# Moving three kinds of stores from SyncE's queue to ScalarE's in a graph network kernel

## The chip, the cores and the metric

The kernel runs on one core of a Trainium2 chip. The metric is the device time of one execution in microseconds (us); the time given for the kernel is the median of several executions, and one further execution was recorded by the hardware profiler. Engines are named as the profile names them: PE (TensorE; PEld is its weight load), DVE (VectorE), ACT (ScalarE), POOL (GpSimd) and SP (SyncE). Each has its own queue of instructions and works through it in order. A DMA is started by an instruction in the queue of SP, ACT or POOL; "SPq" and "ACTq" mark such rows in a timeline.

## The reference, cut to what matters

Four graph layers work on 6250 nodes with 256 features each and 106250 edges sorted by destination. Each adds its result to its input and normalizes the rows.

```python
edge_index = jnp.stack([src, dst])
x = _layernorm(x + _L0_gnn_ref(x, edge_index, L0_gnn_weight, L0_gnn_attn_l, L0_gnn_attn_r), axis=-1)
x = _layernorm(x + _L1_gnn_ref(x, L1_gnn_W, edge_index), axis=-1)
x = _layernorm(x + _L2_gnn_ref(x, edge_index, edge_weight, L2_gnn_W1, L2_gnn_b1, L2_gnn_W2, L2_gnn_b2), axis=-1)
x = _layernorm(x + _L3_gnn_ref(x, L3_gnn_W, edge_index), axis=-1)
```

The first is an attention over single edges. The other three are of the form "multiply the node features by a matrix, scale, gather the row of each edge's source, add it up at the destination, scale". The third does this twice. So there are four aggregations; the last one aggregates at the source and is taken as a dense product with the adjacency matrix of the graph.

## The kernel before, in words

Nodes are cut into 49 blocks of 128, edges into 831 tiles of 128. The function `sorted_edges` holds everything that follows; its order is written out by hand (`tc.manual_schedule()`), so each engine runs its instructions in the order in which the Python code emits them. Generators are used to interleave parts: each `yield` marks a place at which another part may put in its instructions.

**The front** (to 266 us) loads, counts degrees, and computes the attention in seven groups of seven blocks. For each group, `end` (L844 on) scales seven blocks on ACT into tiles `h0` (L856), of which there are four, and stores each as 128 rows of the first table in HBM, `tables[0]` (L857); then ACT writes the normalized blocks in place (L860), and one store of the whole group follows (L862). ACT also takes the square root of each group (L310) and the exponential (L825), whose function tables are loaded in between.

**Aggregation** (`aggregate`) is called for three layers, here called layers 0, 1 and 2. It runs over steps of four edge tiles: 155 steps in layer 0, 208 in each of the others. In a step POOL starts four gathers (L953), each bringing 128 rows of a table into one of 16 tiles `g`. PE multiplies each with a one-hot tile into `agg` (L960). ACT copies that to `part` (L963). In the next step, PE multiplies `part` with a second one-hot tile (L924), and DVE adds the result into a ring of accumulators (L929). When a block of nodes is complete, a `finish` generator runs on it: matrix product (L305), scaling, normalization on DVE with a square root on ACT (L310). In layer 0, `rest1` ends with a store of the normalized block (L1078, on SP), a scaling on ACT into `row` (L1081) and the store of `row` into the second table, `tables[1]` (L1082).

**Beside layers 0 and 1** runs `build`, which makes the dense adjacency matrix block by block. Per step of the aggregation it is advanced 2.75 times (layer 0) or 2.95 times (layer 1). It has two kinds of pieces. `count` makes one-hot tiles on DVE (L503, L506), multiplies them on PE into PSUM tiles `pa` (L527), which ACT casts into one of two tiles, `AT` and `big` (L531), while DVE adds up a count from the same PSUM tile (L533). `use` takes the finished block: for the last 13 blocks of nodes it first multiplies it with the table in dense form (L547, 147 matmuls in seven pieces), then it turns the block in ten pieces of up to five 128x128 tiles: PE transposes into a PSUM tile `tp` (L559), ACT copies it to one of three tiles `ac` (L563), and a DMA stores 160 KB into `adj` in HBM (L564). The tiles `pa`, `tp` and one more kind share three PSUM buffers; the function `behind` puts off the emptying of each until the next piece has been emitted, so ACT empties one while PE fills the next. The blocks that need the dense product come first in `order`, so all of them fall into layer 0.

Loads of the kernel's own rows (`fetch`, L991), of edges for `build` (L434) and all stores but POOL's are in SP's queue, in the order of emission. All DMAs of SP and ACT take turns on eight semaphores, and each waits until the one before it on its semaphore has landed.

**Layer 2** has the dense product with `adj` beside it (L1195, loads L1165) and a tail of dense products alone. The layers are tied together by their tables: the first gather of a layer waits until all stores of its table have landed.

Of the kernel before, what the change touches and what calls it, by code (L numbers as in the profile page):

```python
# [23 lines left out]
P = 128  # L24
# [219 lines left out]
def sorted_edges(ctx, gr, x, src, dst, edge_weight, w0, attn_l, attn_r, w1, w2a, b2a, w2b, b2b, w3,  # L244
# [8 lines left out]
    V, S, G, T, SY = nc.vector, nc.scalar, nc.gpsimd, nc.tensor, nc.sync  # L253
# [28 lines left out]
    tables = [dram.tile([NP, D], F32, name=f"h{i}") for i in range(3)]  # L282
# [3 lines left out]
    adj = dram.tile([NB, P, NP], BF, name="adj")  # L286
# [26 lines left out]
    def rsqrt_end(y, d, s):  # L313

        V.reciprocal(y, s)
        V.tensor_mul(s, y, y)
        V.tensor_mul(s, s, d)
        V.tensor_scalar(s, s, -0.5, 1.5, op0=OP.mult, op1=OP.add)
        V.tensor_mul(y, y, s)
# [92 lines left out]
    def build(bg, ps, more, finish_dense):  # L412
# [70 lines left out]
        def behind(empty=None):  # L483
            while pending:
                pending.pop(0)()
            if empty:
                pending.append(empty)
# [50 lines left out]
        def use(b, AT):  # L538

            behind()  # L540
            if b >= NS1:
                while not parted:
                    yield
                acc = ps.tile([P, D], F32, name="da", bufs=1)
                for k in range(NB):
                    for j in range(3):
                        T.matmul(acc, AT[:, k, :], HP[:, k, j, :], start=k == 0 and j == 0,  # L547
                                 stop=k == NB - 1 and j == 2)
                    if k % SB == SB - 1:
                        yield  # L550
                more.append(finish_dense(b, acc))

            V.tensor_add(AT[:, b, :], AT[:, b, :], ident_b)

            for k0 in sorted(range(0, NB, KC), key=lambda k: k <= b < k + KC):
                n = min(KC, NB - k0)
                tp = ps.tile([P, KC, P], BF, name="tp", tag="w", bufs=3)
                for k in range(n):
                    T.transpose(tp[:, k, :], AT[:, k0 + k, :], ident_b)  # L559

                def empty(tp=tp, k0=k0, n=n):
                    ac = bg.tile([P, KC, P], BF, name="ac", bufs=3)
                    S.copy(ac[:, :n, :], tp[:, :n, :])  # L563
                    SY.dma_start(adj[b, :, k0 * P:(k0 + n) * P], ac[:, :n, :].rearrange("p k q -> p (k q)"))  # L564

                behind(empty)
                yield
# [36 lines left out]
    with one_order:  # L604

        with tc.tile_pool(name="first", bufs=1) as ft, \
# [186 lines left out]
            row = ft.tile([1, P], F32, name="row")  # L793
# [50 lines left out]
            def end(i, mv, va, s):  # L844

                rs = wk.tile([P, GB, 2], F32, name="rstd")
                sh = wk.tile([P, GB, 2], F32, name="sh")
                rsqrt_end(rs[:, :, 0], va, s)
                V.scalar_tensor_tensor(sh[:, :, 0], mv[:, :, 0], -1.0, rs[:, :, 0], op0=OP.mult, op1=OP.mult)
                d = dis1[:, i * GB:(i + 1) * GB]  # L850
                V.tensor_mul(rs[:, :, 1], rs[:, :, 0], d)
                V.tensor_mul(sh[:, :, 1], sh[:, :, 0], d)
                for j in range(GB):
                    b = i * GB + j
                    h = wk.tile([P, D], F32, name="h0", bufs=4)
                    S.activation(h, X[:, b, :], AF.Identity, bias=sh[:, j, 1:2], scale=rs[:, j, 1:2])  # L856
                    SY.dma_start(tables[0][b * P:(b + 1) * P, :], h)  # L857
                for j in range(GB):
                    b = i * GB + j
                    S.activation(X[:, b, :], X[:, b, :], AF.Identity, bias=sh[:, j, 0:1],  # L860
                                 scale=rs[:, j, 0:1])
                SY.dma_start(xs[0][i * GB * P:(i + 1) * GB * P, :].rearrange("(b p) d -> p b d", p=P),  # L862
                             X[:, i * GB:(i + 1) * GB, :])
# [6 lines left out]
            for i in range(ng):  # L870
                if i + 3 < ng:
                    gather_ext(i + 3)
                if i + 2 < ng:
                    gather_alt(i + 2)
                zm = begin(i)
                if last:
                    end(*last)
                last = i, *middle(i, *zm)
            end(*last)

        with tc.tile_pool(name="acct", bufs=1) as ap, tc.tile_pool(name="gat", bufs=16) as gat, \
# [163 lines left out]
            def normalized(y):  # L1045
                mv, va = norm_begin(y, 1)
                yield
                s = rsqrt_begin(va, [P, 1])
                yield
                norm_end(y, y, 1, mv, va, s)  # L1050
# [22 lines left out]
            def rest1(b, ph, xr):  # L1073
                y = fin.tile([P, 1, D], F32, name="y", bufs=3)
                V.scalar_tensor_tensor(y[:, 0, :], ph, dis1[:, b:b + 1], xr, op0=OP.mult, op1=OP.add)
                taken.pop()
                yield from normalized(y)
                SY.dma_start(xs[1][b * P:(b + 1) * P, :], y[:, 0, :])  # L1078
                yield
                row = fin.tile([P, D], F32, name="row")  # L1080
                S.activation(row, y[:, 0, :], AF.Copy, scale=dis2[:, b:b + 1])  # L1081
                SY.dma_start(tables[1][b * P:(b + 1) * P, :], row)  # L1082

            def finish1(b):
                assert weighed
                xr, o = fetch(xs[0], b, "xr"), own(b)
                yield
                yield from bank()
                ph = sums(b, W1)
                yield  # L1090
                yield from rest1(b, ph, xr)
                yield from follow(b, o)

            def finish_dense(b, acc):
                xr = fetch(xs[0], b, "xr")
                a = fin.tile([P, D], F32, name="h")
                S.copy(a, acc)
                yield
                xT = yield from transposed(a)
                yield from bank()  # L1100
                ph = times(ps, xT, W1, tag="ep")
                yield
                yield from rest1(b, ph, xr)
                joined.append(b)
# [543 lines left out]
```

## Time and profile before

| | us |
|---|---|
| median of 3 runs | 3590.57 |
| the runs | 3584.35 to 3593.58 |
| the profiled execution | 3590.18 |
| its span, first to last instruction | 3588.3 |
| first gather of layer 0 | 266.3 |
| last gather of layer 0, first of layer 1 | 1118.7, 1135.5 |
| last adjacency store | 2168.1 |
| last gather of layer 1 | 2216.0 |
| last gather of layer 2 | 3280.5 |

The page of the profile gives the busy time of each engine, the same in 40 slices of the span, the DMA queues, the chain of work that ended last, and the costliest groups of instructions. A group's line names the line of code, the engine, the operation, what is written from what, the shape and how often; after the first bar stand the busy time and the mean duration of one in ns, after the second the idle time of the engine just before them and what ended it. A line of waits names who waited for whom, then the sum in us, how many times, and the longest. A line of a timeline has its start, its length in us, engine, line and operation, and in brackets the idle time before it and what ended that. DMA-issuing instructions are not counted as busy.

### The profile page before, as it was taken

Reading aid. Unit: us, or ns where it says so; the run is one execution under the profiler, and the core shown is the slowest. Engines: PE = TensorE matmul, PEld = TensorE weight load, DVE = VectorE, ACT = ScalarE, POOL = GpSimd, SP = SyncE. Lnnn points to the kernel's source line nnn. Section 1 sums busy time; section 2 is a strip of 40 time slices with the busy share of each in tenths; the row PEclk is TensorE's granted clock in tenths of the full one; section 3 lists DMA queues with packets and bytes.
Section 4 is the critical chain, followed back from the end, with each engine's and each line's share of the span. In section 5 each row is a group of like instructions: output and inputs, shape, how many; then the busy total and the mean of one; then the engine's idle time right before and its main releaser. Section 6 shows DMA issues by size and latency. Waiting matters only on the chain.

```text
span 3588.3 us, 64967 instructions
## 1 busy us (share of the span) xinstructions
PE 2824.3 (79%) x22576; PEld 1987.6 (55%) x22576; DVE 1965.7 (55%) x6286; ACT 1057.4 (29%) x2424; POOL 2382.0 (66%) x2424
## 2 busy tenths in 40 slices
PE   5607679999997777777777775588898888889998
PEld 4402356666664444444444443366677676667887
DVE  4575876565667767676767662234444334333333
ACT  1261343333335444444444441121111111111000
POOL 3657467777776777777777776777777777774000
PEclk7558789999999989999989995599999999999999
DMA  5244455555555555555555554477777777665554
GB/s 150 64 155 119 133 162 160 159 165 158 171 173 165 166 162 168 164 164 166 166 164 164 164 164 146 118 248 247 246 243 237 239 234 228 214 203 179 174 185 136
DMA packets 390822, 630.21 MB, mean 176 GB/s; under 512 B 67788, under 2 KB 299603, under 8 KB 390453
## 3 DMA queue, kind: packets, MB, share of 16 engines
q0 software_dynamic: 114288, 307.59, 30.5%
q1 hardware_dynamic: 275090, 315.19, 26.7%
q8 instruction: 179, 2.93, 0.3%
q10 hardware_dynamic: 1104, 3.19, 0.2%
q14 instruction: 161, 1.31, 0.1%
HBM read 469.36 MB, written 157.64 MB: 175 GB/s over the span
## 4 chain that ended last, share of the span: by engine, by line
PE 36%; DMA 20%; issue 6%; DVE 3%; POOL 2%; ACT 2%; SPq 1%; DVEq 0%; ACTq 0%; POOLq 0%
DMA g<-h,e_srci 18%; PE acc L1195 18%; PE agg L960 6%; PE pa L527 5%; PE agq L924 2%; POOL g L953 2%; PE mm L305 2%; PE tp L559 1%; ACT ac L563 1%; PE own L1014 1%; DMA adj<-ac 1%; DMA xr<-x 1%; SPq L434 1%; PE da L547 0%; SPq L430 0%
## 5 line engine op out<-in xcount | busy, mean ns | idle before, releaser
L953 POOL DMA_INDIRECT g<-h,e_srci x2282 | 2240.9, 982 | 773.5 <-issue 328.9
L1195 PE MATMUL acc<-XP,ad 128*128 128x256 bf16 x7203 | 849.8, 279 | 6.1 <-DMA ad<-adj 6.1
L1195 PEld LDWEIGHTS <-ad 128*128 128x128 bf16 x7203 | 704.1, 100 | 182.0 <-issue 82.8
L527 PE MATMUL pa<-ok,olb 128*128 128x400 bf16 (+1 forms) x2352 | 574.9, 372 | 144.7 <-ACT ac L563 73.1
L960 PE MATMUL agg<-g,oh 128*32 128x256 f32 x4564 | 402.5, 427 | 316.7 <-DMA g<-h,e_srci 315.8
L963 ACT COPY part<-agg 128x256 f32<-128x256 f32 x571 | 212.3, 372 | 1487.0 <-PE agg L960 1468.3
L929 DVE TENSOR_TENSOR ACCT<-ACCT,agq 128x128 f32 x571 | 163.8, 287 | 882.2 <-PE agq L924 878.3
L527 PEld LDWEIGHTS <-olb 128*128 128x128 bf16 x2352 | 221.1, 103 | 405.8 <-issue 176.3
L506 DVE TENSOR_SCALAR ok<-it,key 128x784 bf16<-128x784 f16 x1176 | 440.7, 432 | 0.0
L924 PEld LDWEIGHTS agq<-oq,part 128*128 128x128 f32 x2284 | 346.0, 206 | 59.3 <-ACT part L963 25.8
L924 PE MATMUL agq<-oq,part 128*128 128x64 f32 x2284 | 352.0, 280 | 14.8 <-ACT part L963 10.4
L563 ACT COPY ac<-tp 128x640 bf16<-128x640 bf16 (+1 forms) x490 | 333.0, 697 | 63.4 <-DMA adj<-ac 49.1
L960 PEld LDWEIGHTS agg<-g,oh 128*32 128x32 f32 x4564 | 93.6, 112 | 385.9 <-DMA g<-h,e_srci 339.3
L533 DVE TENSOR_TENSOR cnt_s<-cnt_s,pa 128x49 f32<-128x49 f32 x392 | 79.4, 203 | 261.7 <-ACT AT L531 147.8
L531 ACT CAST AT<-pa 128x400 bf16<-128x400 f32 (+1 forms) x400 | 192.1, 499 | 92.6 <-PE pa L527 90.9
L503 DVE TENSOR_TENSOR olb<-it,key 128x384 bf16<-128x384 f16 x392 | 216.7, 553 | 4.5 <-issue 4.3
L531 ACT CAST big<-pa 128x400 bf16<-128x400 f32 (+1 forms) x384 | 183.5, 501 | 90.9 <-PE pa L527 89.3
L380 PE MATMUL pc<-oh,sel_f 128*17 128x392 f32 x136 | 48.8, 510 | 120.7 <-DVE oh L374 120.7
L559 PEld LDWEIGHTS <-AT 128*128 128x128 bf16 x1225 | 86.6, 103 | 95.6 <-issue 81.1
L559 PEld LDWEIGHTS <-big 128*128 128x128 bf16 x1176 | 83.4, 104 | 88.4 <-issue 72.0
L559 PE MATMUL tp<-ident_b,AT 128*128 128x128 bf16 x1225 | 113.5, 231 | 23.0 <-ACT ac L563 20.9
L310 ACT ACTIVATE rs<-va 128x1 f32<-128x1 f32 (+2 forms) x118 | 24.8, 210 | 358.5 <-DVE va L332 358.3
(265 smaller groups left out, 2897.9 us busy)
## 6 DMA issues: line engine op xcount, KB each, us to landing
adj<-ac SPq DMA_DIRECT2D x441, 160.0 KB
ad<-adj SPq DMA_DIRECT2D x96, 640.0 KB
g<-h,e_srci POOLq DMA_INDIRECT x2282
l<-pre SPq DMA_DIRECT2D x60, 512.0 KB
pre<-l SPq DMA_DIRECT2D x60, 512.0 KB
own<-h SPq DMA_DIRECT2D x147, 128.0 KB
xr<-x SPq DMA_DIRECT2D x98, 128.0 KB
x<-y SPq DMA_DIRECT2D x98, 128.0 KB
```

The lines of the kernel that those rows point to most:

```text
L503: V.tensor_tensor(t, it[:, None, :n].to_broadcast([P, CAP, n]), key[:, k, :, None].to_broadcast([P, CAP, n]), op=OP.is_equal)
L506: V.tensor_scalar(ok[:, i, :KW], it, key[:, 0, i:i + 1], None, op0=OP.is_equal)
L527: T.matmul(pa[:, :c - c0 * GR], ol[:, j, :], ok[:, j, c0 * GR:c], start=j == 0, stop=j == CAP - 1)
L531: S.copy(AT[:, c0:c1, r * GR:(r + 1) * GR], pa[:, :m].rearrange("p (k g) -> p k g", g=GR))
L559: T.transpose(tp[:, k, :], AT[:, k0 + k, :], ident_b)
L563: S.copy(ac[:, :n, :], tp[:, :n, :])
L924: T.matmul(p2[:, h, :], part[:m, h * P:(h + 1) * P], oq[:m, q % 2, :], start=True, stop=True)
L929: V.tensor_add(ACT_[:, :, ds(c, WQ)], ACT_[:, :, ds(c, WQ)], p2)
L953: G.indirect_dma_start(out=g, out_offset=None, in_=table, in_offset=bass.IndirectOffsetOnAxis(ap=e_srci[:, t:t + 1], axis=0))
L960: T.matmul(p1[j * W:(j + 1) * W, :], hots[q // 2][0][:, q % 2 * Q4 + j, :], gs[j], start=True, stop=True)
L963: S.copy(part[:n * W, :], p1[:n * W, :])
L1195: T.matmul(acc[:, k, :], ad[:, (b - b0) % BC, k * P:(k + 1) * P], HP[:, b, j, :], start=b == b0 and k % 2 == 0 and j == 0, stop=b == b1 - ...
```

## The change

Three store instructions are given to another queue, each to that of the engine whose instruction stands just ahead of it in the code. Data, sizes, buffers and the order of emission stay as they are. On ACT, 588 DMA-issuing instructions are added (490 of L564, 49 of L857, 49 of L1082), and SP's queue has as many fewer. PE, DVE and POOL have the same instructions in the same order.

```diff
                 def empty(tp=tp, k0=k0, n=n):
                     ac = bg.tile([P, KC, P], BF, name="ac", bufs=3)
                     S.copy(ac[:, :n, :], tp[:, :n, :])
-                    SY.dma_start(adj[b, :, k0 * P:(k0 + n) * P], ac[:, :n, :].rearrange("p k q -> p (k q)"))
+                    S.dma_start(adj[b, :, k0 * P:(k0 + n) * P], ac[:, :n, :].rearrange("p k q -> p (k q)"))
...
                     h = wk.tile([P, D], F32, name="h0", bufs=4)
                     S.activation(h, X[:, b, :], AF.Identity, bias=sh[:, j, 1:2], scale=rs[:, j, 1:2])
-                    SY.dma_start(tables[0][b * P:(b + 1) * P, :], h)
+                    S.dma_start(tables[0][b * P:(b + 1) * P, :], h)
...
                 row = fin.tile([P, D], F32, name="row")
                 S.activation(row, y[:, 0, :], AF.Copy, scale=dis2[:, b:b + 1])
-                SY.dma_start(tables[1][b * P:(b + 1) * P, :], row)
+                S.dma_start(tables[1][b * P:(b + 1) * P, :], row)
```

## The prediction

> **What bounds the kernel now.** I read the page's busy times and slices first, then its cost groups, then waits and windows stage by stage, because the average shares mix stages with different limits.
>
> ```profile
> PE 2824.3 (79%) x22576; PEld 1987.6 (55%) x22576; DVE 1965.7 (55%) x6286; ACT 1057.4 (29%) x2424; POOL 2382.0 (66%) x2424
> L953 POOL DMA_INDIRECT g<-h,e_srci x2282 | 2240.9, 982 | 773.5 <-issue 328.9
> L563 ACT COPY ac<-tp 128x640 bf16<-128x640 bf16 (+1 forms) x490 | 333.0, 697 | 63.4 <-DMA adj<-ac 49.1
> ```
>
> POOL's 66% hides a gap of 0.30 us after each gather: 2282 x (0.982 + 0.30) = 2926 us of a 3588 us span. Gathers, four to a step of the aggregation loop, run from 266 us to 3281 us, so this is the pacemaker unless something else holds it. The window table says where that is (columns: PE, PEld, DVE, ACT, POOL busy, granted clock, DMA share, GB/s).
>
> ```profile
> 450.00:1118.00 668.00, 597.35 (x5086) 423.55 (x5086) 422.52 (x1506) 265.73 (x632) 497.80 (x507) 0.97 0.57 166
> 1135.00:2170.00 1035.00, 766.44 (x5791) 450.67 (x5791) 707.72 (x2261) 481.32 (x1034) 792.90 (x794) 0.90 0.56 165
> ```
>
> Layer 0 (first row): 507 gathers x 0.30 + 497.8 = 650 of 668 us; PE is busy for 89%. Layer 1 (second): 794 x 0.30 + 792.9 = 1031 of 1035, so POOL is full, with PE at 74%. Who waits for whom in the two windows, layer 0 in the first fence, layer 1 in the second:
>
> ```profile
> POOL g L953 <- PE agg L960: 33.1, 56, 3.9
> PE tp L559 <- ACT ac L563: 19.9, 13, 3.5
> PE pa L527 <- ACT ac L563: 17.3, 24, 1.9
> ACT ac L563 <- DMA adj<-ac: 15.8, 8, 5.6
> ```
>
> ```profile
> PE agg L960 <- DMA g<-h,e_srci: 168.2, 118, 3.6
> PE pa L527 <- ACT ac L563: 53.7, 99, 1.6
> ```
>
> In layer 0 POOL waits for PE to free a gather buffer (33.1 us, of which 56 x 0.30 is the ordinary gap), and PE never has a gather wait of note: PE's queue, and what PE waits for, sets the pace. In layer 1 PE waits 168 us for gathers. I also compared each step's first gather with the matmul that freed the buffer it takes (16 gathers back): the margin has a median of 2 to 5 us with minima of 0.3 in layer 0, and 12 to 13 us in layer 1. After 2168 us there is no store of the moved kinds; layer 2 and the dense tail have nothing to change.
>
> **The change, part by part.** 490 adjacency stores (L564), 49 rows of the first table (L857) and 49 of the second (L1082) leave SP's queue and enter ScalarE's, each behind the instruction that made its data. No other engine's order changes.
>
> *What SP loses* is worth little. SP issued them in 0.32 us (median) and otherwise waited for ScalarE (788.5 us for `ac`); SP is no bound. What its order did cost is lateness: behind a store of a normalized row (L1078) that waits for VectorE, adjacency stores went out over 1 us late for 31 of 156 copies before 1118 us, and ScalarE then waited for a buffer: the 15.8 us above (49.1 in all, the other 33.3 in layer 1). A store issued right behind its copy lands after 2.6 us (median here, 4.0 at the 95th percentile), and its buffer is wanted three copies later, over 4 us on. I let all 15.8 us go.
>
> *What ScalarE gains.* The timeline of one step with two transposed tiles, layer 0:
>
> ```profile
> 714.11 0.35 ACT L963 COPY part<-agg 128x256 f32<-128x256 f32 x1
> 714.36 1.29 ACT L563 COPY ac<-tp 128x640 bf16<-128x640 bf16 x2
> 715.08 0.91 SPq L564 DMA_DIRECT2D adj<-ac  x2
> 715.11 0.71 PE L527 MATMUL pa<-ok,olb 128*128 128x433 bf16 x3 [1.18 <-ACT ac L563]
> 715.53 0.90 ACT L531 CAST big<-pa 128x400 bf16<-128x400 f32 x2
> 715.70 0.44 PE L559 MATMUL tp<-ident_b,AT 128*128 128x128 bf16 x5
> ```
>
> Two copies of 0.70 us take 1.29 because the second starts 0.59 after the first; the casts follow just as closely. With a store between, the next instruction waits for the copy's end (0.11 lost), 0.026 until the issue (as SP's row shows), 0.34 for the issue (mean of the 490 rows on SP) and about 0.06 to start again (the step from a wait row to its copy at 1086.4 us): **0.54 us per store**. Bounds: the issue alone, 0.32; and 0.8, if it takes on ScalarE twice the 0.36 us of its one comparable store (L754). Two rules of the Trainium skill bear here. "DMA: Bandwidth & Descriptors" (Issuing engines are not separate DMA queues) says that queues of different engines end on the same 16 DMA engines and that spreading them saves only issue time, usually small beside the transfer. By that rule, 0.32 beside 2.6 us, the change is worth about nothing and the time stays 3591; but the rule weighs an issue against its transfer, and here it is weighed against a step in which PE already waits for ScalarE. "Perfetto Trace Analysis" (DMA Instruction — HWDGE) has the semaphore wait of such a DMA in the sequencer, while computing instructions wait in a queue of their own: nothing behind the store is made ready. That speaks for 0.54 against 0.34; with 0.34, layer 0's sum below would be 30 us and not 48.
>
> *Layer 0, on the path.* Of 129 steps in the window (from one step's first L960 matmul to the next), 41 have no `ac` copy and run the dense matmuls L547 (6.23 us each, PE full); 33 have one copy; 55 have two or three (4.34 us for the 49 without dense matmuls). Behind the first store stand the second `ac` copy, two casts and the next `part`. PE's second transposition at 715.70 starts 0.05 after the second copy ends, so it comes 0.54 later: 55 x 0.54 = 30 us. With one copy, the casts and `xT` come later, and only part of that reaches PE (VectorE's count L533 waits for the casts, the own-matmul for `xT`): half, 33 x 0.27 = 9. Of 43 row stores 35 fall into steps with copies, where the row can stand just ahead of `part`: half again, 9. Together 48, against nothing if PE's other waits cover all, and 103 if every one of 144 + 47 stores passes on fully. Less 15.8 for the ended buffer waits, less 3 of margin at the gathers, plus 4 for the 18 stores of 400 to 450 us, where PE is behind too: **+33 us**, from -16 to +91.
>
> *Ahead of layer 0.* The last group of seven rows runs from 257.54 to 261.47 us (3.93), and POOL's first instruction of the layer (265.08) waits for the ScalarE pass behind it. With 0.59 + 0.026 + 0.32 + 0.06 = 1.0 each, seven take 7.0: +3.1, and the buffer waits of 0.36 go inside it. The groups before have the same +3.1, of which idle time at the next square root covers 1.28 and 1.93 us (its waits at 242.85 and 255.85); earlier ones end in a 6.5 us wait for gathers and cost nothing. Two groups carry about 3 to the last: **+6 us**, 0 to 9.
>
> *End of layer 0.* From the last gather (1118.71) to the next layer's first (1135.48) POOL waits for the last row store, issued at 1132.84, right after its row, as it would be from ScalarE. A few adjacency stores in that chain: **+1**.
>
> *Layer 1: nothing.* 329 stores x 0.54 = 178 us at the very most, over 201 steps 0.88 each; PE's wait for gathers is 0.84 per step and 12 us stand in the buffers. Without that cover each 0.1 us per step costs 20 us.
>
> *Waits that the change could add.* Eight DMA semaphores go round all stores and loads of both queues in program order, so a store on ScalarE waits for the landing of the eighth DMA before it, often SP's. In this trace that DMA had landed at least 0.96 us before each of the 526 stores after 450 us (median 6 and more), and 6.7 before the earlier ones, so I take 0. Behind it would be queued everything that feeds PE.
>
> Sum: 6 + 33 + 1 = 40. 3588.3 + 40 = 3628; the profiled execution took 1.9 beyond its span and was 0.4 below the median: **3631 us**.
>
> **Rivals.**
> *Hidden anyway.* PE's waits in layer 0 cover the stores, and POOL's own pitch (650 of 668 us) sets the layer; only the front pays. For: POOL is within 18 us of full. Against: PE's margin is used up at minima of 0.3 us. 3591 + 6 = 3597.
> *The buffer waits were the price.* ScalarE idles 235 us in layer 0 waiting for `agg`, so issues fall into idle time and only the ended 15.8 us count, the front being absorbed too: 3591 - 16 = 3575. It decides when less than about a sixth of the 103 us reaches PE. Against: the copies stand back to back just where PE waits for them.
> *A dearer issue.* At 0.8 us per store and full passing, layer 1's steps need 5.2 - 0.84 + 1.6 x 0.8 = 5.64 us against POOL's 5.19: +90 there, layer 0 half as much again (+55): about 3740. With half passing, layer 1 is still hidden.
> That the stores stay on SP is excluded by the order of instructions: 588 of them stand in ScalarE's queue.
>
> **How the numbers follow.** 0.3% (11 us) is about what a measurement here can tell from no change. Chances: likeliest case 0.65 (its own range 3612 to 3660: 0.34 us per store and less passing, or 70% passing), hidden 0.14, faster 0.10, dearer 0.11. Slower by over 0.3%: 0.65 + 0.11 and a little of the hidden case, 0.78; same 0.12; faster 0.10. The range leaves out the faster case and the upper part of the dearest: 3595 to 3675.
>
> **What would show it.** Right: `pa` and `tp` waits for `ac` in layer 0 well above 37 us; steps with two copies near 4.9 us; the `ac` wait for `adj` near 0; first gather near 272 us, the layer's last near 1157; layer 1's length within 5 us of 1081; POOL waiting longer for `agg`. Wrong: a layer 0 not longer, ScalarE waiting at a store for another DMA, a store issue far from 0.34 us, or layer 1 no longer held by POOL.

## The result, and the profile after

The changed kernel takes 3637.95 us (median of 4 runs, 3627.68 to 3640.35), the kernel before 3591.84 (median of 4) on the same chip. The estimated ratio is 1.0133, 95% interval 1.0111 to 1.0155, or 48 us (40 to 56) more; the two medians lie 46 apart. The prediction was 3631 us.

The page of the changed kernel, the three lines that were shown of before:

```profile
PE 2841.5 (78%) x22576; PEld 1994.1 (55%) x22576; DVE 1965.9 (54%) x6286; ACT 1090.2 (30%) x2424; POOL 2395.4 (66%) x2424
L953 POOL DMA_INDIRECT g<-h,e_srci x2282 | 2255.2, 988 | 806.2 <-issue 325.9
L563 ACT COPY ac<-tp 128x640 bf16<-128x640 bf16 (+1 forms) x490 | 338.1, 690 | 49.6 <-ACT ac L563 22.5
```

POOL's idle time before gathers has gone from 773.5 to 806.2 us. A copy into `ac` costs what it did (690 ns against 697), but no longer waits for its buffer's store: what it waits for most is now the copy ahead of it on its own engine, which is a wait that the kernel before did not have.

The profiled execution took 3640.35 us with a span of 3638.6, 50.3 more than before. By the times of the first and last gathers, the 50.3 are:

| stretch | before | after | difference |
|---|---|---|---|
| to the first gather of layer 0 | 266.3 | 269.4 | +3.1 |
| layer 0, first to last gather | 852.4 | 888.6 | +36.2 |
| gap to layer 1 | 16.8 | 18.3 | +1.5 |
| layer 1 | 1080.6 | 1088.4 | +7.8 |
| gap, layer 2 and tail | 1372.2 | 1373.8 | +1.6 |

Layer 0 and layer 1 in the table of windows (columns as before: PE, PEld, DVE, ACT, POOL busy, granted clock, DMA share, GB/s):

```profile
453.00:1158.00 705.00, 613.98 (x5082) 431.51 (x5081) 421.92 (x1501) 275.23 (x630) 500.49 (x506) 0.94 0.54 156
1176.00:2265.00 1089.00, 794.10 (x5918) 462.78 (x5919) 717.00 (x2289) 501.20 (x1043) 835.63 (x831) 0.89 0.55 162
```

Layer 0 is 37 us longer with the same work in it. PE's idle time there is 705 - 613.98 = 91.0 us, where it was 70.7 (+20.4), and PE's busy time itself has grown by 16.6, with the granted clock at 0.94 instead of 0.97. Layer 1 is 8 us longer, and POOL's busy time has grown by as much (the window of before in the prediction is narrower; over 1135 to 2216 us POOL was busy for 827.7, by a row shown below).

Who waits for whom in layer 0 after the change, 453 to 1158 us, POOL and PE first, ScalarE in the second fence:

```profile
POOL g L953 <- PE agg L960: 70.7, 73, 4.2
...
PE pa L527 <- ACT ac L563: 16.1, 23, 1.7
PE tp L559 <- ACT ac L563: 15.7, 16, 2.4
PE mm L305 <- ACT xT L1040: 11.9, 11, 1.7
PE tp L559 <- DVE cnt_s L533: 9.7, 5, 2.4
PE pa L527 <- DVE cnt_s L533: 8.8, 13, 3.4
...
PE tp L559 <- ACT big L531: 4.7, 11, 0.5
PE own L1014 <- ACT h L1097: 4.4, 6, 1.4
PE tp L559 <- ACT AT L531: 3.8, 10, 0.5
```

```profile
ACT AT L531 <- ACT ac L563: 11.9, 29, 0.7
ACT ac L563 <- ACT ac L563: 9.9, 22, 0.5
```

And before, 450 to 1118 us, the lines of PE that neither the prediction nor this text has shown yet:

```profile
PE pa L527 <- DVE cnt_s L533: 9.8, 12, 3.6
...
PE mm L305 <- ACT xT L1040: 3.9, 9, 0.9
PE tp L559 <- DVE cnt_s L533: 2.6, 2, 2.0
...
PE own L1014 <- ACT h L1097: 1.4, 3, 0.5
```

POOL waits more than twice as long for PE to free a gather buffer (33.1 us before). The waits point to ScalarE: casts and copies now stand still behind the copy ahead of them. But PE's waits for `ac` itself have not grown: 31.8 us against 37.2. The lateness reaches PE by what ScalarE does after the copies: the wait for `xT` has gone from 3.9 to 11.9 us, the two for the count `cnt_s` together from 12.4 to 18.5, that for `h` from 1.4 to 4.4; the waits of `tp` for the casts, 4.7 us for `big` and 3.8 for `AT`, were not among those of before. Together these have grown by about 25 us; less the 5.4 of `ac`, this is about the 20.4 us of new idle time.

In layer 1, 1176 to 2265 us, PE still waits for gathers first (168.2 us before, in the narrower window):

```profile
PE agg L960 <- DMA g<-h,e_srci: 174.6, 113, 4.5
```

Last the timeline of a step with two copies (start, length, engine, line):

```profile
724.04 0.70 ACT L563 COPY ac<-tp 128x640 bf16<-128x640 bf16 x1
724.77 0.33 ACTq L564 DMA_DIRECT2D adj<-ac  x1
...
725.19 0.69 ACT L563 COPY ac<-tp 128x640 bf16<-128x640 bf16 x1 [0.45 <-ACT ac L563]
725.91 0.33 ACTq L564 DMA_DIRECT2D adj<-ac  x1
725.93 0.44 PE L559 MATMUL tp<-ident_b,AT 128*128 128x128 bf16 x5 [0.43 <-ACT ac L563]
```

The copy ends at 724.74, the store goes out at 724.77 and takes 0.33, the next copy starts 1.15 us after the first one did instead of 0.59: 0.56 us per store. This step is no exception: in layer 0 the 38 pairs of copies that follow each other start 1.15 us apart in the median, the 33 pairs of before 0.58. All 588 stores go out 0.03 us after the end of the instruction that made their data, and of 513 stores on ScalarE from 460 to 2200 us not one lies beside a running instruction of ScalarE.

### The profile page after: what moved, and what is told of

The parts are those of the page before. It is cut to its first block, busy times and chain, and to the rows that moved or that the text cites. A ratio compares the mean times of both kernels' runs of the same rounds, so it can differ in the third digit from the quotient of the medians.

```text
span 3638.6 us, 64214 instructions
## 1 busy us (share of the span) xinstructions
PE 2841.5 (78%) x22576; PEld 1994.1 (55%) x22576; DVE 1965.9 (54%) x6286; ACT 1090.2 (30%) x2424; POOL 2395.4 (66%) x2424
## 4 chain that ended last, share of the span: by engine, by line
PE 50%; DMA 20%; DVE 7%; issue 7%; ACT 5%; POOL 2%; ACTq 1%; SPq 0%; DVEq 0%; POOLq 0%
DMA g<-h,e_srci 18%; PE acc L1195 18%; PE agg L960 8%; PE pa L527 8%; PE da L547 6%; PE agq L924 4%; PE mm L305 3%; ACT ac L563 2%; POOL g L953 2%; PE tp L559 2%; PE pc L380 1%; DMA xr<-x 1%; DVE ok L506 1%; PE own L1014 1%; ACT AT L531 1%
## 5 line engine op out<-in xcount | busy, mean ns | idle before, releaser
L953 POOL DMA_INDIRECT g<-h,e_srci x2282 | 2255.2, 988 | 806.2 <-issue 325.9
L1195 PE MATMUL acc<-XP,ad 128*128 128x256 bf16 x7203 | 849.3, 279 | 6.2 <-DMA ad<-adj 6.2
L1195 PEld LDWEIGHTS <-ad 128*128 128x128 bf16 x7203 | 703.6, 100 | 181.0 <-issue 81.3
L527 PE MATMUL pa<-ok,olb 128*128 128x400 bf16 (+1 forms) x2352 | 588.0, 379 | 152.4 <-ACT ac L563 74.2
L960 PE MATMUL agg<-g,oh 128*32 128x256 f32 x4564 | 403.4, 428 | 305.6 <-DMA g<-h,e_srci 304.5
L960 PEld LDWEIGHTS agg<-g,oh 128*32 128x32 f32 x4564 | 93.8, 113 | 374.0 <-DMA g<-h,e_srci 323.0
L531 ACT CAST AT<-pa 128x400 bf16<-128x400 f32 (+1 forms) x400 | 184.7, 488 | 134.4 <-PE pa L527 90.5
```

The costliest lines, as they stand in the source:

```text
L527: T.matmul(pa[:, :c - c0 * GR], ol[:, j, :], ok[:, j, c0 * GR:c], start=j == 0, stop=j == CAP - 1)
L531: S.copy(AT[:, c0:c1, r * GR:(r + 1) * GR], pa[:, :m].rearrange("p (k g) -> p k g", g=GR))
L953: G.indirect_dma_start(out=g, out_offset=None, in_=table, in_offset=bass.IndirectOffsetOnAxis(ap=e_srci[:, t:t + 1], axis=0))
L960: T.matmul(p1[j * W:(j + 1) * W, :], hots[q // 2][0][:, q % 2 * Q4 + j, :], gs[j], start=True, stop=True)
L1195: T.matmul(acc[:, k, :], ad[:, (b - b0) % BC, k * P:(k + 1) * P], HP[:, b, j, :], start=b == b0 and k % 2 == 0 and j == 0, stop=b == b1 - ...
```

## The experiments

Four sets of runs, each on one chip together with the kernel before. On two of the four chips the kernel before took about 4475 us instead of 3590; what is measured there is compared only there. In the tables, layers 0 and 1 are the times from the first to the last gather in the one profiled execution of each kernel.

**One kind of store at a time, on a chip with another pace.** Each of the first three makes one of the three edits of the change: e1_adj that of L564, e2_h0 that of L857, e3_row that of L1082. The fourth moves no store and only takes ScalarE's time.

```diff
# e4_pad
                     S.copy(ac[:, :n, :], tp[:, :n, :])
+                    S.copy(ac[:, :2, :], ac[:, :2, :])
```

> Only the 490 adjacency stores (L564) move to ScalarE; both kinds of table rows stay on SP. Theory 'time on ScalarE' (each store holds ScalarE for about half a us, and in layer 0 PE has to wait for it): of the 36 us that layer 0 grew in the changed kernel, about 28 here, the front 0, so about 3591 + 30 to 38 = 3621 to 3629. Rival 'the rows do it' (row stores stand just ahead of the copy to part, which PE needs next): less than 15 us over the kernel before. Layer 1 is 1081 us from first to last gather if the 8 us that it grew in the changed kernel were chance, 1088 if the adjacency stores on ScalarE's queue made them.

> Only the 49 rows of the first table (L857) move. First gather at 269.4 us instead of 266.3, as in the changed kernel, and nothing behind it: 3591 + 3 = 3594, not to be told from the kernel before. The prediction had 6 us for this part; if the two earlier groups of seven rows had really carried their delay over, the first gather would come at 272.

> Only the 49 rows of the second table (L1082) move. Theory 'time on ScalarE': 34 of them stand in steps with copies, at half a us and half passing on: layer 0 +9, in all 3600. If the copy to part never waits for a row store, or PE has it late anyway: 3591. Rival 'the rows do it': over 3610.

> All stores stay on SP; after each copy into ac ScalarE copies 256 of its columns onto themselves, which holds ScalarE about as long as issuing a store (0.06 to start, some 0.4 us), and the store waits for it. Theory 'time on ScalarE': layer 0 grows by as much as with the adjacency stores moved or more, since the waits for late stores stay: 3591 + 30 to 50. Rival 'the queue' (what costs is ScalarE's own DMA ring, two queues that share the engines or the eight semaphores): within 10 us of the kernel before. Layer 1 stays at 1081 us by the rival reading of its 8 us as an effect of the queue, and by chance too; 1088 if mere time on ScalarE makes them.

Measured against 4473.94 us (4440.82 to 4499.19) of the kernel before on this chip:

| | median, us | ratio (95%) | layer 0, us | layer 1, us |
|---|---|---|---|---|
| e1_adj | 4440.26 | 0.9930 (0.9907 to 0.9953) | 1063.8 | 1368.3 |
| e2_h0 | 4477.74 | 1.0011 (0.9992 to 1.0029) | 1089.7 | 1374.2 |
| e3_row | 4462.47 | 0.9979 (0.9958 to 1.0000) | 1082.6 | 1380.1 |
| e4_pad | 4462.11 | 0.9984 (0.9959 to 1.0009) | 1078.7 | 1384.9 |

All the expectations started from a layer 1 that POOL paces at 1.30 us per gather. Here it is not so. The gathers' row of e2_h0 over layer 1:

```profile
L953 POOL DMA_INDIRECT g<-h,e_srci x831 | 831.2, 1000 | 570.8 <-PE agg L960 250.2 <-issue 160.7 <-PE pa L527 50.0
```

and that of the kernel before on the chip on record:

```profile
L953 POOL DMA_INDIRECT g<-h,e_srci x830 | 827.7, 997 | 268.2 <-issue 116.1 <-PE pa L527 55.8 <-PE agg L960 25.9
```

A gather takes 1.000 us as elsewhere, but POOL idles 570.8 us before 831 of them, 0.69 each and not 0.32, at least 300 us of it waiting for PE. So none of the expectations on the whole time can be held against these runs, and they do not decide between the theories for the case on record. They do show that the sign is another here: moving the adjacency stores gains 0.7%. The front can be compared: from the first exponential, which stands ahead of all the stores moved, to the first gather it takes 112.5 us in e2_h0 and 108.7 in e1_adj, 3.8 more where 3 were expected.

**Adjacency stores by layer, and two ways to keep them late.** On another chip, with the kernel before at 3583.77 us (3573.17 to 3597.09).

```diff
# e5_adj_l0 (the 16 blocks that are made in layer 0 or at its start; e6_adj_l1 has SY and S the other way round)
-                    SY.dma_start(adj[b, ...
+                    (S if b >= NS1 - 2 or b == 0 else SY).dma_start(adj[b, ...
# e7_defer (all stay on SP; the two stores of rest1 are emitted one to one and a half steps later)
-                SY.dma_start(xs[1][b * P:(b + 1) * P, :], y[:, 0, :])
+                later.append([3, lambda: SY.dma_start(xs[1][b * P:(b + 1) * P, :], y[:, 0, :])])
-                SY.dma_start(tables[1][b * P:(b + 1) * P, :], row)
+                later.append([2, lambda: SY.dma_start(tables[1][b * P:(b + 1) * P, :], row)])
# e8_late (adjacency alone on ScalarE, each store issued behind the next copy)
-                    SY.dma_start(adj[b, ...
+                    if held:
+                        held.pop()()
+                    held.append(lambda: S.dma_start(adj[b, ...
```

> Adjacency stores of the first 16 blocks (those of layer 0) on ScalarE, all later ones and all rows on SP. Theory: layer 0 grows by about 28 us and layer 1 stays at 1081, so 3591 + 28 to 30 = 3620. If layer 1 grew in the changed kernel because of what layer 0 leaves behind, it is 1088 here too.

> The reverse: the first 16 blocks' stores on SP, the later 33 blocks' stores (layer 1) on ScalarE, rows on SP. Theory: POOL's gathers set layer 1, so the stores are hidden: layer 0 as before (852 us from first to last gather), the time 3591. If DMAs issued by ScalarE lengthen the gathers (1.006 us mean against 0.997 in layer 1 of the changed kernel), layer 1 is 1088 us and the time 3599.

> All stores on SP; the stores of normalized rows (L1078) and of the second table's rows (L1082) are emitted one to one and a half steps later, when their data are ready, so that the adjacency stores behind them in SP's queue are not late. ScalarE's waits for ac buffers in layer 0 (15.8 us) go to near 0. If they were on the path, as the prediction took them: 3591 - 10 to 16, and somewhat more where PE's granted clock rises; if they only took the place of other waits: 3591.

> Adjacency stores on ScalarE, rows on SP, but each store is issued one piece later, ahead of the copy after next in emission, when the copy that it waits for has long ended. The issue itself (0.33 us) stays, the lost overlap and the wait for the copy's end (about 0.15 us) go. By the prediction's sum (0.54 per store, of which 0.34 issue) about a third of what the adjacency stores cost is gone: 8 to 12 us under the run with the plain move. If the issue alone is what counts, the same as the plain move; if waiting in the sequencer is what counts, near the kernel before.

| | median, us | ratio (95%) | layer 0, us | layer 1, us |
|---|---|---|---|---|
| e5_adj_l0 | 3604.18 | 1.0057 (1.0038 to 1.0076) | 867.2 | 1081.2 |
| e6_adj_l1 | 3586.86 | 1.0003 (0.9993 to 1.0014) | 853.0 | 1084.0 |
| e7_defer | 3583.05 | 1.0002 (0.9991 to 1.0013) | 844.6 | 1084.5 |
| e8_late | 3583.21 | 0.9997 (0.9984 to 1.0009) | 848.5 | 1082.0 |

The adjacency stores of layer 0 cost 20 us (14 to 27), somewhat less than the 28 to 30 expected, and the more numerous ones of layer 1 nothing (1 us, -3 to 5). Counting layer 0's steps from one first matmul of L960 to the next, the 52 steps with two copies and no dense matmul take 4.80 us in e5_adj_l0 and 4.43 before.

e7_defer tests the gain that was counted against these costs. It empties SP's queue of the stores that block it, and ScalarE's wait for an `ac` buffer in layer 0 falls from 15.8 us to:

```profile
ACT ac L563 <- DMA adj<-ac: 5.3, 3, 3.2
```

Ten microseconds of waiting are gone on ScalarE, and the time is the same: a gain of more than 3 us is outside the interval. (Layer 0 is 8 us shorter in this one profiled execution, layer 1 is 4 longer.) So most of these waits lay beside other waits and were worth nothing.

e8_late has the same adjacency stores in ScalarE's queue as the changed kernel has, and costs nothing, where a gain of only 8 to 12 us on the plain move was thought likeliest. Its timeline (copies joined in one row):

```profile
713.66 1.29 ACT L564 COPY ac<-tp 128x640 bf16<-128x640 bf16 x2
714.39 0.33 ACTq L567 DMA_DIRECT2D adj<-ac  x1
...
714.83 0.90 ACT L532 CAST big<-pa 128x400 bf16<-128x400 f32 x2
```

Two copies again take 1.29 us, as in the kernel before, and the issue of 0.33 runs beside the second one. In this step the store still waits for the first copy: that ends at 714.36, and the store goes out 0.03 us later. But the second copy, which starts at about 714.25, was handed to ScalarE ahead of the store, so the engine is at work while its queue waits and issues.

**Rows alone, ScalarE's time alone, and all three kinds late.** A third chip, the kernel before at 3585.54 us (3571.25 to 3594.93). e9_row and e10_pad are e3_row and e4_pad again. e11_next is the changed kernel with every store issued one ScalarE instruction later (fence cut to the main lines):

```diff
+    held = []
+    def flush():
+        while held:
+            held.pop(0)()
+    class Behind:                      # in place of S for copies and activations
+        def copy(self, *a, **k):
+            S.copy(*a, **k)
+            flush()
...
-                    SY.dma_start(adj[b, ...
+                    held.append(lambda: S.dma_start(adj[b, ...
-                    SY.dma_start(tables[0][b * P:(b + 1) * P, :], h)
+                    held.append(lambda h=h, b=b: S.dma_start(tables[0][b * P:(b + 1) * P, :], h))
-                SY.dma_start(tables[1][b * P:(b + 1) * P, :], row)
+                held.append(lambda: S.dma_start(tables[1][b * P:(b + 1) * P, :], row))
```

> Only L1082, the 49 rows of the second table, on ScalarE; the rest on SP. The prediction gave these 9 us (35 rows beside copies, half of 0.54 us each). After the result, the steps of layer 0 with a row are 0.66 us longer than those without in the changed kernel (5.47 against 4.81 us), where they were 0.28 longer before, so rows may cost more than that: theory now, layer 0 (first to last gather) +12 to +25 us, and ratio 1.003 to 1.007. If rows cost what the prediction gave them: +5 to +10 and ratio 1.001 to 1.003. If they cost only beside adjacency stores (both on ScalarE): 0 within 4 us, ratio 0.999 to 1.001. Layer 1 within 3 us of before in all cases.

> All stores stay on SP; behind each copy of a turned tile ScalarE copies 256 of its columns onto themselves, which waits for the copy's end and holds ScalarE 0.3 to 0.4 us, about what a store does, with no DMA in its queue. If it is ScalarE's time behind the copy's end that costs (theory): layer 0 +12 to +40 us (adjacency stores alone cost about 15, and here the store on SP also goes out 0.35 us later), ratio 1.003 to 1.012. If it is something of the DMA in ScalarE's queue: layer 0 within 5 us of before and ratio 0.999 to 1.002.

> All three kinds of store on ScalarE as in the changed kernel, but each issued one ScalarE instruction later: behind the next copy, cast or activation and not behind the one that made its data. Same number of DMAs in ScalarE's queue. Theory (the cost is the wait in the queue for data that was made just ahead, not the issue): layer 0 within 6 us of before, first gather within 1 us, ratio 0.996 to 1.002; a version that could beat both, since the 15.8 us of waits for a buffer of turned tiles in layer 0 go to about half. If the issue itself costs 0.33 us of ScalarE (rival): layer 0 +15 to +30, ratio 1.005 to 1.010.

| | median, us | ratio (95%) | layer 0, us | layer 1, us |
|---|---|---|---|---|
| e9_row | 3590.26 | 1.0019 (1.0009 to 1.0029) | 853.2 | 1082.0 |
| e10_pad | 3607.34 | 1.0052 (1.0034 to 1.0071) | 868.8 | 1085.8 |
| e11_next | 3585.36 | 1.0000 (0.9987 to 1.0013) | 851.3 | 1076.0 |

e9_row missed the theory of that moment (12 to 25 us): rows alone cost 7 us (3 to 10), what the prediction had given them. The steps of the changed kernel with a row and two copies, 5.47 us, had misled me; with rows alone they take 4.83 us (4.62 before), and those with two copies and no row 4.22 (4.34 before). Layer 0 of its profiled execution is no longer than before, so where the 7 us lie is not shown.

e10_pad moves no store, but holds ScalarE for 0.40 us (its 146 self-copies in layer 0) plus the wait for the copy's end: two copies in a row start 1.04 us apart. It costs 19 us (12 to 25), as e5_adj_l0 does. So nothing of the DMA in the queue is needed to explain what the adjacency stores cost: ScalarE's time behind the copy is enough.

e11_next has the same 588 stores in the same queue as the changed kernel, and its time is that of the kernel before. Its layer 0 in the windows, a wait of layer 0, and the timeline of a step:

```profile
450.00:1111.00 661.00, 590.76 (x5093) 420.28 (x5086) 417.43 (x1494) 272.47 (x628) 498.98 (x503) 0.98 0.57 166
```

```profile
ACT ac L262 <- DMA adj<-ac: 1.8, 3, 1.0
```

```profile
714.21 1.19 ACT L262 COPY ac<-tp 128x640 bf16<-128x640 bf16 x2
...
714.94 0.33 ACTq L580 DMA_DIRECT2D adj<-ac  x1
...
715.31 0.20 ACT L266 ACTIVATE rs<-va 128x1 f32<-128x1 f32 x1
715.43 0.33 ACTq L580 DMA_DIRECT2D adj<-ac  x1
```

(L262 and L266 are the helper that stands for ScalarE's `copy` and `activation`.) All 522 stores on ScalarE from 460 to 2200 us lie beside a running instruction of ScalarE; in the changed kernel none of 513 does. Nor is it that the stores have nothing left to wait for: 419 of the 588 go out within 0.06 us of the end of the instruction that made their data, so their turn had come before. What differs is the one instruction that ScalarE was given ahead of them. From the first exponential to the first gather it takes 109.3 us (108.7 before, 112.8 in the changed kernel). The waits for `ac` buffers have gone as well, from 15.8 to 1.8 us, and again no gain can be measured. So no version here beats the kernel before; e11_next undoes the change's cost and no more.

**Both kinds of layer 0 together.** e12_adj_row moves L564 and L1082 and leaves L857 on SP, to see whether the parts add up.

> The changed kernel but for the first table's rows: L564 (adjacency) and L1082 (rows of the second table) on ScalarE, L857 on SP. Measured one at a time on this chip against the kernel before: adjacency of layer 0 1.0057, of layer 1 1.0003, rows 1.0019. If they add up: 1.0079 (interval about 1.006 to 1.010), layer 0 +18 to +25 us in the profile. If both together cost more than their sum, because a row's issue then stands in the same queue as the copies' and each lands on a ScalarE that is already late: the changed kernel's 1.0133 less the front's 4.9 us, 1.0115 to 1.013, layer 0 +30 to +40 us, with row steps beside two copies near 5.4 us as in the changed kernel (4.83 with rows alone).

It came to a chip on which the kernel before takes 4478.85 us (4452.24 to 4513.52), and took 4448.36 there: 0.9931 (0.9907 to 0.9956), layer 0 1051.0 us. That is the gain that e1_adj has on the other chip of this pace, and it says nothing about the sum on the chips of 3590 us. The question is left open.

## Why the prediction was right, and where it was not

The direction, the range and the likeliest case held: 3637.95 against 3631, a cost of 48 us against 40. Step by step:

**0.54 us per store**: 0.56 in the timeline, with issues of 0.33. The rival of a dearer issue (0.8 us) is out. Of the two rules weighed, the one of "Perfetto Trace Analysis" (DMA Instruction — HWDGE) decided rightly: the semaphore wait of such a DMA stands in the sequencer, and an instruction behind it has to wait too (0 of 513 stores beside a running instruction), while one that was handed over ahead of it runs on (522 of 522 in e11_next). The rule of "DMA: Bandwidth & Descriptors" (Issuing engines are not separate DMA queues), that another issuing engine only saves issue time and that this is small, fits e11_next (1.0000), and misses the changed kernel by the wait.

**Adjacency in layer 0**: the terms for two copies (30), one copy (9), ended buffer waits (-15.8), margin (-3) and 400 to 450 us (+4) come to 24 us; e5_adj_l0 measured 20 (14 to 27). The net is right, by two errors that cancel. "I let all 15.8 us go" was counted as a gain of 15.8: e7_defer ends 10 of them with no store on ScalarE, and gains nothing. And two copies cost 4.80 - 4.43 = 0.37 us per step and not 0.54, 19 us in 52 steps; steps with one copy, no row and no dense matmul show no cost (3.51 us in 12 steps against 3.67 in 11). Part of each store lies beside other waits of PE. The two small terms, -3 and +4, were not tested.

**Rows in layer 0**: 9 us; e9_row 7 (3 to 10). **Front**: 6 us; 4, from the first exponential to the first gather (112.8 us against 108.7). Seven rows take 6.63 us and not 7.0, where they took 4.0, and the earlier groups add 1.5 and not 3. **End of layer 0**: 1; 1.5.

**Layer 1**: 0. By e6_adj_l1 right, 1 us (-3 to 5). The profiled execution of the changed kernel is outside the 5 us named (+7.8), all of it in the length of the gathers, 1.006 us each against 0.997, with the gap after them unchanged at 0.305. That length differs from execution to execution without regard to the stores: 1.003 in e10_pad, where none is moved, and 0.992 in e11_next, where all are. What sets it is open.

**Waits that the change could add**: 0, and right: all 588 stores go out 0.03 us after their data's end, so none waited for the landing of another DMA.

**The signs**: steps with two copies and no dense matmul take 5.05 us (4.9 named), the last gather of layer 0 came at 1158.0 (1157), the `ac` wait for `adj` is gone from the list, and POOL waits longer for `agg`. The sign "waits for `ac` well above 37 us" was wrong: they fell to 31.8. The path was taken to lead from copy to PE by the next `tp` or `pa`; it led mostly by the casts, the counts and `xT`. The prediction had half of a one-copy step's cost come that way and all of a two-copy step's directly. Once PE has waited elsewhere, it reaches `pa` and `tp` later and finds `ac` done.

**The sum**: measured one by one, 20 + 1 + 7 + 4 = 32 us, and all together 48, with some 12 us of uncertainty in the difference (the halves of the four intervals, added as squares). If the 16 us are real, they are what the prediction has no term for: it counts PE's waits, and not the clock. Of the 37 us by which layer 0 is longer in its profile, only 20.4 are PE's idle time; 16.6 are longer busy time. From 184 us behind the first gather to the end of layer 0, TensorE's clock is at half for 82 us, against 42 in the kernel before, 44 in e5_adj_l0 and 31 in e9_row, and 40 us more at half speed are some 20 us of work lost. This is not one execution alone: over the span the granted clock is 0.884 to 0.891 in all four of the changed kernel (mean 0.888), and in the mean 0.894 in 88 of the kernel before on the two other chips of this pace, 0.894 in e5_adj_l0 and 0.892 in e9_row. An estimate of the time at half clock from these (twice the missing share, times the span) is 812 us against 756, 764 and 774. That PE's longer waits bring the clock down is likely, but not shown: the run that was to tell, e12_adj_row, could not. So it is partly luck that +33 us for layer 0 came so close to +36.

The rivals: "hidden anyway" (3597) holds for layer 1 and not for layer 0. "The buffer waits were the price" (3575) fell twice: less than a sixth of the 103 us would have had to reach PE, and by the single runs (20 + 7 us) about a quarter did; and the price itself proved to be next to nothing (e7_defer).

## What to carry to other kernels

A store that stands right behind the instruction that makes its data, in the queue of an engine that others wait for, costs that engine the wait for the end of the instruction, the issue and the restart: 0.56 us here for an issue of 0.33. Put one more instruction of that engine between them and it costs nothing (588 stores, ratio 1.0000), even where the store still has to wait for its data (419 of the 588): the engine has work while its queue waits and issues. A wait that a change ends is a gain only if the engine that waits sets the pace there; take it from the sum only after having looked for who waits for that engine.

## What the runs showed of the hardware that was not expected

**The clock goes to half without a long pause.** A stretch of the changed kernel's layer 0 in three windows, and PE's wait in the first:

```profile
1069.80:1073.20 3.40, 0.90 (x10) 0.56 (x12) 3.30 (x11) 0.00 (x0) 0.31 (x1) 1.00 0.36 110
1073.20:1080.00 6.80, 6.44 (x37) 3.92 (x30) 4.08 (x16) 2.28 (x7) 4.16 (x5) 0.50 0.37 110
1080.00:1083.40 3.40, 3.22 (x31) 1.97 (x29) 2.04 (x7) 2.40 (x5) 2.67 (x3) 1.00 0.49 140
```

```profile
PE own L1014 <- DVE y L1075: 2.5, 1, 2.5
```

PE was busy for 0.90 of 3.40 us, with a longest pause of 2.5, and then ran 6.8 us at half clock. In the six traces looked at (before, changed, e5_adj_l0, e9_row, e10_pad, e11_next) every half-clock spell from 480 to 1110 us follows 3.41 us in which PE was busy for 27 to 62%, with no pause above 2.5 us; spells are multiples of 3.4 us, 12 of them in the changed kernel and 6 before. The Trainium skill ("TensorE: Matmul & The Clock Gate", Part 1) has the clock fall after at least one idle window of some 3.4 us; here a window that is only sparsely filled was enough. On the grid of 3.41 us that these spells keep, every window at full clock in which PE was busy for less than 44% was followed by half clock, none above 62% was, and between the two both occur. Idle time alone does not tell how often: e5_adj_l0 and e10_pad have 85 us of it in layer 0, nearly the 91 of the changed kernel, and 44 us at half clock.

**Chips differ in pace.** The same kernel took 3584 to 3592 us in three sets of runs and 4474 to 4479 in two, with gathers of the same length and more than twice the gap between them (0.69 us against 0.32 in layer 1, by the two rows shown), and a granted clock of 0.81 over the span against 0.89. The instructions themselves take the same time at the same clock: the matmul of L1195 has a median of 273 ns at full clock and 421 at half, in e2_h0 as in the kernel before. But PE, VectorE and ScalarE stand still more often with nothing to wait for that the profile shows ("issue"). In layer 0 of e2_h0, 530 to 1390 us, PE has waits that the list of the kernel before does not have:

```profile
PE tp L559 <- issue: 33.5, 15, 4.2
```

Over the span such idle time of PE (pauses above 0.15 us) comes to 429 us, against 0 in the kernel before. Where it comes from was not tried, and neither why moving the adjacency stores gains 0.7% there, twice (e1_adj, e12_adj_row).
